# Moving the two transposes of 47 node sets of a graph network layer from TensorE to a DRAM round trip and VectorE block turns

## The chip, the cores and the metric

The kernel runs on one core of a Trainium2 chip. The metric is the time on the device of one execution, in microseconds (us). The engines of the core are TensorE (PE in the profile, with its weight loads as PEld), VectorE (DVE), ScalarE (ACT), GpSimd (POOL) and SyncE (SP, which here only issues DMA transfers and reads numbers into its registers). Each engine works through its own list of instructions in order and waits on semaphores.

## The reference

The reference is one layer of a graph network with 6250 nodes of 256 features and 206250 edges, sorted by target node.

```python
h = jnp.maximum(_layernorm(x, axis=-1), 0.0)
polarity = jnp.clip(edge_attr[:, 0:1], 0.0, 1.0)
raw = edge_attr[:, 1:]
e = jax.nn.relu(raw @ W_e1.T + b_e1) @ W_e2.T + b_e2
edge_emb = (e * (polarity + 0.01)) @ W_le.T + b_le
msg = jax.nn.relu(h[src] + edge_emb)
aggr = jax.ops.segment_sum(msg, dst, num_segments=N)
g = (h + aggr) @ W_g1.T + b_g1
hn = (g - mean(g)) * rsqrt(var(g) + 1e-5) * ln_g + ln_b
out = x + relu(hn) @ W_g2.T + b_g2
```

All of it is in 32-bit floats. For each node the last three lines need the node's row turned twice: TensorE contracts over partitions, so `h + aggr` (nodes on partitions) must be turned to features on partitions ahead of the product with `W_g1`, and the normalised rows must be turned again ahead of the product with `W_g2`.

## The kernel before

Edges are worked on in tiles of 128. Two tiles make a unit; I call the work of one unit a **step**. Twelve steps make a group of 3072 edges, and there are 67 groups and a remainder. The order of all instructions is written out by a Python loop over the steps (`for u in range(LEAD, NU)`), which emits for each step, to all engines, what is due; each engine then runs its own list in that order.

In a step TensorE makes the second product of a unit (line 377, eight instructions, since a 32-bit product counts twice) into a bank of PSUM that ScalarE has filled with the offset (line 408). VectorE multiplies by the polarity and adds the gathered source rows (line 822, two instructions for a unit), and ScalarE takes the relu (line 833). GpSimd gathers the source rows by indirect DMA (line 740). In the last step of a group TensorE also makes the first layer of the edges of the next group (line 342; VectorE and ScalarE take it out of PSUM at lines 355 and 358) and the sums of the whole group by target node (line 873). ScalarE and VectorE put the sums together in `ms` (lines 893 and 894), and SyncE writes them to the DRAM tensor `sum_d` (`rows_out`, line 980, four copies, two of which are emitted one step after the group's end and two one step later).

A **node set** is 128 nodes. When the sums of all its groups are written, `far_work` does the rest for it, spread over the steps behind: load the node's rows and the sums (line 1013), add them (line 1016), and then six stages, put on a list by `at(now + ...)`: `turned` (two transposes on TensorE, line 177, copied from PSUM by ScalarE at line 181), `one` (product with `W_g1`, line 192, then VectorE's addition and statistics at lines 200 to 163), `rooted` (ScalarE, line 206), `normed` (VectorE, lines 211 and 212), `two` (two transposes on TensorE, line 218, and relu with `ln_g` and `ln_b` by ScalarE, line 222) and `three` (product with `W_g2`, line 231, addition at line 236, and the copy out at line 239). 47 node sets go this way: 42 with buffers of their own, five with buffers that were kept free (`msg` in the names); in the last three of these five, the fillers, `two` and `three` are left for the very end. The two last node sets go another way (`node_work`), with one turn on TensorE each.

What `soon(n, fn)` puts off runs at the end of exactly the step asked for, all of it; what `at(u, fn)` puts off runs one piece for a step, and not in the last or first step of a group.

The first 24 units are kept (`KEPT`) and finished later. Ten of them have their source rows from the start; of the others, `BY_ROW` units get their source rows row by row, through copies of 1 KB that SyncE issues after it has read the row numbers into registers (lines 777 and 782, four rows in every second step), and the rest by gathers of GpSimd that stand between the others.

Of the kernel before, what the change touches and what calls it, by code (L numbers as in the profile page):

```python
# [9 lines left out]
F32 = mybir.dt.float32  # L10
I32 = mybir.dt.int32
AF = mybir.ActivationFunctionType
# [5 lines left out]
P = 128  # L18
# [29 lines left out]
ROWS = 4  # L48
BY_ROW = 5
SEEDS = 3  # L50
# [54 lines left out]
def gnn_kernel(ctx: ExitStack, tc: tile.TileContext, x, src_c, src_r, dst_c, dst_r, pol_c, raw_t, w_e1t, w_e2,  # L105
# [64 lines left out]
    def finish_nodes(nd, ps, w, n):  # L170
# [44 lines left out]
        def second(hs):  # L215
# [9 lines left out]
            return nT, a  # L225

        def third(nT, xt):
            nT, a = nT
# [20 lines left out]

        return turn, first, root, scaled, second, third, load_x, offset  # L250

# [3 lines left out]
    with fast:  # L255
# [216 lines left out]
        w0 = early.enter_context(tc.tile_pool(name="w0", bufs=1))  # L472
        wle_s = w0.tile([P, 2, D], F32, name="wle_s")
        nc.sync.dma_start(out=wle_s, in_=vec(w_let))
        we2_s = w0.tile([P, 2, D], F32, name="we2_s")
        nc.scalar.dma_start(out=we2_s, in_=vec(w_e2))
# [20 lines left out]
        dst_f = w0.tile([P, NT], F32, name="dst_f")  # L497
        be2_b = w0.tile([P, 2, P], F32, name="be2_b")

# [114 lines left out]


        wg1_s = const.tile([P, 2, D], F32, name="wg1_s")
        wg2_s = const.tile([P, 2, D], F32, name="wg2_s")
# [84 lines left out]
        with tc.tile_pool(name="hg", bufs=1) as hg_p, tc.tile_pool(name="ms", bufs=4) as ms_p, \  # L702
                tc.tile_pool(name="sel2", bufs=6) as sel2_p, tc.tile_pool(name="ab", bufs=2) as ab_p, \
                tc.tile_pool(name="nh", bufs=2) as nh, tc.tile_pool(name="nd", bufs=3) as nd, \
                tc.tile_pool(name="nk", bufs=1) as nk:
            base_i = nk.tile([1, NG * S], I32, name="base_i")
# [246 lines left out]
            whole_units = {}  # L953
            ready, fillers = [], []
            left = {w: set(groups_of(w)) for w in range(NW) if groups_of(w)[-1] < FAR}
# [45 lines left out]
            def far_work(w, nd=nd, nh=nh, ab_p=ab_p, filling=False):  # L1001

                box = {}
                turn, first, root, scaled, second, third, load_x, offset = finish_nodes(nd, ps, w, P)

# [9 lines left out]
                def add(i):  # L1015
                    nc.vector.tensor_add(box["h"], box["h"], box["ab"][:, i, :])
# [44 lines left out]
            def node_work(w, spread_now=False):  # L1061
# [4 lines left out]
                far_apart = (3, 5, 4) if gs[-1] < NG - 3 else (2, 3, 2)  # L1066
                turn, first, root, scaled, second, third, load_x, offset = finish_nodes(nd, ps, w, n)

# [205 lines left out]
def any_order(tc, dram, v):  # L1274
# [7 lines left out]
    with tc.tile_pool(name="sc", bufs=1) as sc, tc.tile_pool(name="sk", bufs=2) as sk, \  # L1282
# [93 lines left out]
        def nodes(w, n):  # L1376
            ac = sk.tile([P, D], F32, name="ac_a")
            nc.sync.dma_start(out=ac[:n], in_=acc_d[bass.ds(w * P, n), :])
            turn, one, root, scaled, two, three, load_x, offset = v["finish_nodes"](sk, Fresh(), w, n)
            xt = load_x()  # L1380
            offset(xt)
            three(two(scaled(root(one(turn(ac))))), xt)
# [68 lines left out]
```

## Time and profile before

| | |
|---|---|
| median of three runs | 2704.74 us (2699.62 to 2708.85) |
| the profiled execution | 2698.25 us, of which 2696.1 us from its first to its last instruction |
| mean granted clock of TensorE | 0.973 |
| busy, of the span | TensorE 94%, weight loads 62%, GpSimd 58%, VectorE 48%, ScalarE 48% |
| moved by DMA | 331.78 MB, 123 GB/s in the mean |

A row of the timeline gives the start, the length, the engine, the line, the operation with what it writes and reads, and how many instructions were merged; in brackets stands how long the engine had been idle ahead of it, and what ended that. A row of the groups gives the count, the busy time (overlaps counted once), the mean length of one in ns, and the idle time ahead of them with what ended most of it. SPq is SyncE's list of DMA issues; its time is the time of issuing, not of the transfer.

### The profile page before, as it was taken

The page shows a single profiled execution, that of the slowest core. Times are in us where ns is not written, and L with a number is a line of the kernel's source. Part 1 is how long each engine was busy: PE and PEld are TensorE (multiplying, and loading weights), DVE is VectorE, ACT ScalarE, POOL GpSimd, SP SyncE. Part 2 cuts the span into 40 slices and gives each one's busy share as a digit, 9 for nine tenths or more (in the row PEclk, how much of TensorE's full clock was granted, in tenths as well). Part 3 has the DMA queues.
Part 4 walks back from the last instruction along what each step waited for, and adds up shares of the span by engine and source line. Part 5 has one row for each costly group of instructions (what it writes and reads, how often), then busy time and mean ns, then how long its engine had stood idle before and what let it go on. Part 6 is the DMA issues. An engine that isn't in the chain of part 4 may idle for free.

```text
span 2696.1 us, 55548 instructions
## 1 busy us (share of the span) xinstructions
PE 2538.4 (94%) x19998; PEld 1664.0 (62%) x19998; DVE 1304.9 (48%) x2984; ACT 1290.8 (48%) x2414; POOL 1557.0 (58%) x1664
## 2 busy tenths in 40 slices
PE   9889999999999999999999999999999999999998
PEld 6455655665665666565666666566656665666665
DVE  6446545444444444444444444444444444545454
ACT  6345544444444444444444445444445444545544
POOL 7655555555555555555565555555555555555652
PEclk9889999999999989999999999999999999999999
DMA  9433434343444434434434444443444444434442
GB/s 296 152 93 115 121 116 128 116 123 114 119 121 123 125 105 125 120 115 119 130 109 123 124 118 121 124 117 117 124 121 120 125 121 122 119 115 128 122 120 58
DMA packets 145846, 331.78 MB, mean 123 GB/s; under 512 B 37129, under 2 KB 73836, under 8 KB 144812
## 3 DMA queue, kind: packets, MB, share of 16 engines
q0 software_dynamic: 76896, 210.08, 27.3%
q1 hardware_dynamic: 67368, 114.79, 13.5%
q10 hardware_dynamic: 1300, 3.29, 0.4%
q8 instruction: 160, 2.62, 0.4%
q14 instruction: 122, 1.00, 0.1%
HBM read 306.25 MB, written 34.08 MB: 126 GB/s over the span
## 4 chain that ended last, share of the span: by engine, by line
PE 78%; issue 10%; DVE 5%; ACT 4%; DMA 1%; POOL 1%; another core or an unknown queue 0%; DVEq 0%; SPq 0%; POOLq 0%; ACTq 0%
PE pz L377 40%; PE pz L342 20%; PE pz L873 14%; DVE hg L822 2%; PE pz L192 1%; ACT hg L833 1%; PE pz L231 1%; DVE hx L822 1%; ACT pz L408 1%; ACT hx L833 1%; POOL hg L740 1%; PE pz L218 1%; DVE hs L212 1%; DMA hx<-hb_d,src_s 0%; PE pz L177 0%
## 5 line engine op out<-in xcount | busy, mean ns | idle before, releaser
L377 PE MATMUL pz<-wc_s,e 128*128 128x256 f32 x6448 | 1450.7, 382 | 4.9 <-ACT pz L408 1.8
L377 PEld LDWEIGHTS pz<-wc_s,e 128*128 128x128 f32 x6448 | 1215.0, 191 | 203.5 <-issue 36.0
L740 POOL DMA_INDIRECT hg<-hb_d,src_s x976 | 927.1, 950 | 683.6 <-issue 210.6
L740 POOL DMA_INDIRECT hx<-hb_d,src_s x606 | 573.8, 947 | 400.5 <-issue 134.9
L342 PE MATMUL pz<-raw,we_s 64*32 64x512 f32 x6448 | 627.9, 642 | 82.2 <-issue 48.7
L822 DVE SCALAR_TENSOR_TENSOR hg<-pz,pol_s,hg 128x256 f32<-128x256 f32 x962 | 413.9, 477 | 414.8 <-issue 225.8
L833 ACT ACTIVATE hg<-hg 128x512 f32<-128x512 f32 x481 | 300.9, 626 | 445.4 <-DVE hg L822 365.9
L342 PEld LDWEIGHTS pz<-raw,we_s 64*32 64x32 f32 x6448 | 155.3, 111 | 510.8 <-issue 350.0
L355 DVE TENSOR_SCALAR e<-pz,vecs 128x512 f32<-128x512 f32 x395 | 284.4, 748 | 356.0 <-remote 184.6
L408 ACT ACTIVATE pz<-bc_s 128x512 f32<-128x512 f32 x782 | 452.7, 585 | 0.0
L358 ACT ACTIVATE e<-pz,vecs 128x512 f32<-128x512 f32 x411 | 266.0, 684 | 331.9 <-remote 161.5
L822 DVE SCALAR_TENSOR_TENSOR hx<-pz,pol_s,hx 128x256 f32<-128x256 f32 x602 | 260.9, 478 | 280.0 <-issue 129.5
L833 ACT ACTIVATE hx<-hx 128x512 f32<-128x512 f32 x300 | 188.0, 627 | 314.1 <-DVE hx L822 266.7
L873 PE MATMUL pz<-hg,sel 64*32 64x256 f32 x3848 | 306.2, 393 | 30.5 <-issue 12.7
L873 PEld LDWEIGHTS pz<-hg,sel 64*32 64x32 f32 x3848 | 133.6, 108 | 161.4 <-issue 141.6
L873 PE MATMUL pz<-hx,sel 64*32 64x256 f32 x2408 | 208.4, 387 | 18.6 <-issue 8.5
L894 DVE TENSOR_TENSOR ms<-ms,pz 128x256 f32<-128x256 f32 x68 | 28.6, 421 | 297.1 <-ACT ms L893 297.1
L893 ACT ACTIVATE ms<-pz 128x256 f32<-128x256 f32 x68 | 26.0, 383 | 274.5 <-PE pz L873 273.6
L873 PEld LDWEIGHTS pz<-hx,sel 64*32 64x32 f32 x2408 | 90.0, 107 | 90.8 <-issue 77.1
L803 DVE SCALAR_TENSOR_TENSOR sel<-iota_w,zero_c,rel 128x256 f32<-128x256 f32 x202 | 92.2, 476 | 0.0
L231 PE MATMUL pz<-wg_s,nT 128*128 128x256 f32 (+1 forms) x176 | 45.3, 380 | 0.0
L192 PE MATMUL pz<-wg_s,hT 128*128 128x256 f32 (+1 forms) x176 | 45.3, 380 | 0.0
(136 smaller groups left out, 698.2 us busy)
## 6 DMA issues: line engine op xcount, KB each, us to landing
raw<-in_raw_t_dram SPq DMA_DIRECT2D x99, 512.0 KB
hg<-hb_d,src_s POOLq DMA_INDIRECT x976
hg<-hb_d SPq DMA_DIRECT2D x768, 1.0 KB
sum_d<-zero_d SPq DMA_DIRECT2D x47, 256.0 KB
ab<-sum_d SPq DMA_DIRECT2D x42, 256.0 KB
hx<-hb_d,src_s POOLq DMA_INDIRECT x606
sum_d<-ms SPq DMA_DIRECT2D x264, 32.0 KB
hx<-hb_d SPq DMA_DIRECT2D x512, 1.0 KB
```

Of the source, the lines that this page charges most:

```text
L192: z = nc.tensor.matmul(ph[:n, 0, :], aT[:, c, :n], wg1_s[:, c, :], start=c == 0 and not bias_by_pe, stop=c == 1)
L231: z = nc.tensor.matmul(po[:n, 0, :], nT[:, c, :n], wg2_s[:, c, :], start=c == 0, stop=c == 1)
L342: z[c] = nc.tensor.matmul(bank[s, c].tile[j * W:(j + 1) * W].rearrange("p a b -> p (a b)"), we1_s[s * F:(s + 1) * F, c * P + j * W:c * P + ...
L355: a = nc.vector.tensor_scalar(e1[b][:, c, :], pe, be1_s[:, c:c + 1], 0.0, op0=ALU.add, op1=ALU.max)
L358: a = nc.scalar.activation(e1[b][:, c, :], pe, AF.Relu, bias=be1_s[:, c:c + 1])
L377: z = nc.tensor.matmul(bank.tile[:, i, :], e1[b][:, c, k:k + P], wc_s[:, c, :], start=not seeded and i == c == 0, stop=c == 1, skip_group_ ...
L408: a = nc.scalar.activation(bank.tile, bc_s, AF.Copy)
L740: g = nc.gpsimd.indirect_dma_start(out=hg[u][:, i, :], out_offset=None, in_=hb_d, in_offset=bass.IndirectOffsetOnAxis(ap=src_s[:, 2 * u + ...
L803: nc.vector.scalar_tensor_tensor(sel[g][:, k * S:k * S + n, :], iota_w.rearrange("p (o w) -> p o w", o=1).to_broadcast([P, n, W]), zero_c, ...
L822: product = nc.vector.scalar_tensor_tensor(hg[u][:, i, :], bank.tile[:, i, :], pol_s[:, 2 * u + i:2 * u + i + 1], hg[u][:, i, :], op0=ALU. ...
L833: done[u] = product, nc.scalar.activation(hg[u], hg[u], AF.Relu)
L873: z = nc.tensor.matmul(acc[g][h][j * W:(j + 1) * W, :], sel[g][h * F:(h + 1) * F, k * S + j, :], m[h * F:(h + 1) * F, j % 2, :], start=k = ...
```

## The change

`far_work` no longer turns on TensorE. `first_out` writes the 128 x 256 rows to one of eight DRAM buffers (`turn_d`); `in_blocks` reads them back by four DMA issues, one for each quarter of the partitions, in pieces of 32 floats (128 bytes), so that in the tile `pm` each 32 x 32 block stands where its turned block belongs; `turned` is one VectorE instruction that turns all 32 x 32 blocks. The same round trip (`second_out`, `in_blocks`, `second_turned`) replaces `two`, and the relu with `ln_g` and `ln_b` then goes from SBUF to SBUF (`relu_of`). The first turn changes for all 47 node sets; the second for 44, since the three fillers keep `two` on TensorE. The two stages that issue DMA are put off by `soon`, the others by `at`. `BY_ROW` is four instead of five, so 1024 rows are copied singly instead of 1280, and one more kept unit is gathered by GpSimd (two indirect DMAs). Two weights and a bias that only the start needs are in a pool that is closed early, which makes room for `pm`.

```diff
-BY_ROW = 5
+BY_ROW = 4
...
+    turn_d = [dram.tile([P, D], F32, name=f"turn_d{i}") for i in range(8)]
...
+        def relu_of(nT):
+            for c in range(2):
+                a = nc.scalar.activation(nT[:, c, :], nT[:, c, :], AF.Relu, bias=lnb_s[:, c:c + 1],
+                                         scale=lng_s[:, c:c + 1])
+            return nT, a
...
+                def out_rows(a):
+                    box["d"] = turn_d[len(turned_rows) % len(turn_d)]
+                    turned_rows.append(w)
+                    nc.sync.dma_start(out=box["d"], in_=a)
+
+                def in_blocks():
+                    box["pm"] = pm.tile([P, 2 * S, W], F32, name="pm")
+                    rows = box["d"].rearrange("(b i) (c a j) -> a i c b j", i=W, a=S, j=W)
+                    for q in range(S):
+                        nc.sync.dma_start(out=box["pm"][q * W:(q + 1) * W].rearrange("i (c b) j -> i c b j", c=2),
+                                          in_=rows[q])
+
+                def blocks_turned(name, pool):
+                    t = pool.tile([P, 2, P], F32, name=name)
+                    nc.vector.transpose(t.rearrange("p c n -> p (c n)"), box["pm"].rearrange("p q j -> p (q j)"))
+                    return t
+
+                def first_out():
+                    at_last(box)
+                    out_rows(box["h"])
+
                 def turned():
-                    at_last(box)
-                    box["hT"] = turn(box["h"], nh, "hT")
+                    box["hT"] = blocks_turned("hT", nh)
...
+                def second_out():
+                    out_rows(box["hs"])
+
+                def second_turned():
+                    box["nT"] = relu_of(blocks_turned("nT", nd))
+
                 def two():
                     box["nT"] = second(box["hs"])
...
-                stages = [turned, one, rooted, normed, two, three]
+                line = [(first_out, 2, True), (in_blocks, 3, True), (turned, 1, False), (one, 1, False),
+                        (rooted, 1, False), (normed, 1, False), (second_out, 2, True), (in_blocks, 3, True),
+                        (second_turned, 2, False), (three, 0, False)]
+                if filling:
+                    line = line[:6]

                 def run(i):
-                    stages[i]()
-                    if i < len(stages) - (3 if filling else 1):
-                        at(now + (2, 1, 1, 2, 3)[i], lambda: run(i + 1))
+                    line[i][0]()
+                    if i < len(line) - 1:
+                        if line[i + 1][2]:
+                            soon(line[i][1], lambda: run(i + 1))
+                        else:
+                            at(now + line[i][1], lambda: run(i + 1))
...
-                    fillers.append(stages[-2:])
-                at(now + 12, lambda: run(0))
+                    fillers.append((two, three))
+                soon(12, lambda: run(0))
```

How the order moves is seen best in one group. Its steps are counted from 0 to 11. On TensorE, before, from the end of a group's sums to the second transposes, behind step 7 of the next group (`pz` with its number is a PSUM bank; the two rows that read one `e_10x` are two steps):

```order
L873 MATMUL pz_151<-hg_874,sel_142 32x256
L377 MATMUL pz_146<-wc_s,e_102 128x256 x4
L377 MATMUL pz_148<-wc_s,e_102 128x256 x4
L177 MATMUL pz_147<-ident,stb 128x128 x2
L377 MATMUL pz_150<-wc_s,e_103 128x256 x4
L377 MATMUL pz_144<-wc_s,e_103 128x256 x4
L192 MATMUL pz_151<-wg_s,hT 128x256 x2
L377 MATMUL pz_149<-wc_s,e_104 128x256 x4
L377 MATMUL pz_145<-wc_s,e_104 128x256 x4
L377 MATMUL pz_146<-wc_s,e_105 128x256 x4
L377 MATMUL pz_148<-wc_s,e_105 128x256 x4
L218 MATMUL pz_147<-ident,hs 128x128 x2
```

And now (lines have moved by 5 to 10: 883 is 873, 384 is 377, 238 is 231, 193 is 192):

```order
L883 MATMUL pz_159<-hg_889,sel_150 32x256
L384 MATMUL pz_154<-wc_s,e_110 128x256 x4
L384 MATMUL pz_156<-wc_s,e_110 128x256 x4
L384 MATMUL pz_155<-wc_s,e_111 128x256 x4
L384 MATMUL pz_158<-wc_s,e_111 128x256 x4
L238 MATMUL pz_157<-wg_s,nT 128x256 x2
L384 MATMUL pz_152<-wc_s,e_112 128x256 x4
L384 MATMUL pz_153<-wc_s,e_112 128x256 x4
L193 MATMUL pz_159<-wg_s,hT 128x256 x2
```

The transposes are gone; the product with `W_g1` has moved from behind step 3 to behind step 5, and behind step 3 now stands the product with `W_g2` of the node set before.

On VectorE, now, from step 1 to the statistics (832 is 822, 813 is 803, 243 is 236, 201 is 200):

```order
L832 SCALAR_TENSOR_TENSOR hx_120<-pz_156,pol_s,hx_120 128x256 x2
L1042 STREAM_TRANSPOSE nT<-pm 128x256
L832 SCALAR_TENSOR_TENSOR hx_119<-pz_155,pol_s,hx_119 128x256 x2
L832 SCALAR_TENSOR_TENSOR hg_891<-pz_158,pol_s,hg_891 128x256 x2
L243 TENSOR_TENSOR ot<-pz_157,xt_8469 128x256
L832 SCALAR_TENSOR_TENSOR hg_892<-pz_152,pol_s,hg_892 128x256 x2
L1042 STREAM_TRANSPOSE hT<-pm 128x256
L832 SCALAR_TENSOR_TENSOR hx_124<-pz_153,pol_s,hx_124 128x256 x2
L201 TENSOR_TENSOR hs<-pz_159,rows_b 128x256
```

The second turn of a set stands behind step 1, the first turn of the next set behind step 4, one step ahead of TensorE's use of `hT`.

On SyncE, now, behind the group's end (990 is 980, 251 is 244, 787 and 792 are 777 and 782):

```order
L251 DMA xt_9185<-in_x_dram 128x256
L990 ISA
L990 DMA sum_d<-ms 32x256
L990 ISA
L990 DMA sum_d<-ms 32x256
L1037 DMA pm<-turn_d_68 32x8x32 x4
L787 TENSOR_LOAD list_5910
L792 ISA
L792 DMA hx_122<-hb_d 1x256
```

The four reads in blocks stand behind the last two of the four copies of the group's sums and ahead of the next four single rows, all on the one list of SyncE; the write to `turn_d_68` was issued at the end of the group before.

More of the change, by code (lines that the diff above doesn't have):

```diff
@@ L248, in offset @@
             nc.vector.scalar_tensor_tensor(xt[:n], xt[:n], zero_c[:n], bg2_b[:n], op0=ALU.add, op1=ALU.add)
-        return turn, first, root, scaled, second, third, load_x, offset
+        return turn, first, root, scaled, second, relu_of, third, load_x, offset
     NU = 2 * NB
@@ L1003, in far_work @@
                 box = {}
-                turn, first, root, scaled, second, third, load_x, offset = finish_nodes(nd, ps, w, P)
+                turn, first, root, scaled, second, relu_of, third, load_x, offset = finish_nodes(nd, ps, w, P)
                 def h_of_x():
@@ L1378, in nodes @@
             nc.sync.dma_start(out=ac[:n], in_=acc_d[bass.ds(w * P, n), :])
[L1379 removed]
+            turn, one, root, scaled, two, _, three, load_x, offset = v["finish_nodes"](sk, Fresh(), w, n)
             xt = load_x()
```

15 lines of the change are left out of this document (9 added, 6 removed).

## The prediction

> I expect the changed kernel to be **slower, about 2770 us**: it takes some 38 us of work off TensorE, and makes TensorE wait, 47 times, for a turn that VectorE reaches too late.
>
> **What bounds the kernel now.** I read the page first: the busy shares and the chain that ended last.
>
> ```profile
> PE 2538.4 (94%) x19998; PEld 1664.0 (62%) x19998; DVE 1304.9 (48%) x2984; ACT 1290.8 (48%) x2414; POOL 1557.0 (58%) x1664
> PE 78%; issue 10%; DVE 5%; ACT 4%; DMA 1%; POOL 1%; another core or an unknown queue 0%; DVEq 0%; SPq 0%; POOLq 0%; ACTq 0%
> ```
>
> TensorE is busy 94% of the span and makes up 78% of the chain. Whatever it need not do is a gain, and whatever it must wait for is a loss, as long as nothing else ends later. So I read one group on its timeline.
>
> ```profile
> 1032.53 0.38 PE L177 MATMUL pz<-ident,stb 128*128 128x128 f32 x2
> 1032.75 3.62 PE L377 MATMUL pz<-wc_s,e 128*128 128x256 f32 x16
> 1036.21 1.03 PE L192 MATMUL pz<-wg_s,hT 128*128 128x256 f32 x4
> 1037.07 7.07 PE L377 MATMUL pz<-wc_s,e 128*128 128x256 f32 x32
> 1044.34 0.44 PE L218 MATMUL pz<-ident,hs 128*128 128x128 f32 x2 [0.20 <-DVE hs L212]
> 1044.62 5.34 PE L377 MATMUL pz<-wc_s,e 128*128 128x256 f32 x24
> ...
> 1071.21 0.38 PE L177 MATMUL pz<-ident,stb 128*128 128x128 f32 x2
> ```
>
> The group takes 1071.21 - 1032.53 = 38.7 us. The last of 16 products starts 3.62 - 0.38 = 3.24 us behind the first, so products start every 0.216 us, and a step of eight takes 1.73 us. There is no gap between rows but the 0.20 us at line 218.
>
> **What the change takes away.** The first transposes start at 1032.53 and the next product at 1032.75: the pair costs 0.22 us. Of the 32 products from 1037.07, the last starts at 1037.07 + 7.07 - 0.38 = 1043.76; the next product starts at 1044.62, where 0.22 would do: the second pair, with its wait for VectorE, costs 0.64 us.
>
> ```profile
> L177 PE MATMUL pz<-ident,stb 128*128 128x128 f32 x84 | 16.0, 273 | 0.0
> L218 PE MATMUL pz<-ident,hs 128*128 128x128 f32 (+1 forms) x88 | 18.9, 297 | 8.2 <-DVE hs L212 3.0 <-issue 1.6 <-DVE rs L211 1.5
> L177 PE MATMUL pz<-ident,msg 128*128 128x128 f32 x10 | 1.9, 272 | 0.0
> L218 PE MATMUL pz<-ident,msg 128*128 128x128 f32 x10 | 2.0, 284 | 0.7 <-ACT ms L893 0.7
> L181 ACT ACTIVATE hT<-pz 128x256 f32<-128x256 f32 x42 | 15.3, 365 | 0.0
> ```
>
> 84 + 10 first transposes are 47 pairs, all removed: 47 x 0.22 = 10.3 us. Of the second, 88 + 10 less four of the last two sets and six of the fillers, 44 pairs go: 44 x 0.64 = 28.2 us. Together **38.5 us**, if TensorE stays the bound. ScalarE's copy at line 181 goes too (15.3 us, off the path); its relu stays, now from SBUF.
>
> **What it adds beside other work.** VectorE gets 91 turns of 128 x 256. No turn is in this trace; the nearest rows are an addition of that size and one of twice the size.
>
> ```profile
> L1016 DVE TENSOR_TENSOR stb<-stb,ab 128x256 f32<-128x256 f32 x84 | 35.0, 416 | 1.3 <-DMA ab<-sum_d 1.1
> L843 DVE TENSOR_TENSOR msg<-msg,bc_s 128x512 f32<-128x512 f32 x7 | 4.8, 682 | 0.0
> ```
>
> I take 0.45 us, between bounds of 0.42 and 0.68: 41 us on an engine that is busy 48%. The turn's own length is paid only where TensorE waits for it, below. [...]
>
> The one more kept unit costs GpSimd two gathers:
>
> ```profile
> L740 POOL DMA_INDIRECT hx<-hb_d,src_s x606 | 573.8, 947 | 400.5 <-issue 134.9
> ```
>
> At 947 ns each they are 1.9 us; GpSimd is idle 42% of the span, and its gathers run ahead of their use. If that cover were gone, these would be the cost. SyncE loses 256 single rows and gets 47 + 44 = 91 writes and 364 block reads.
>
> ```profile
> 1025.48 1.62 SPq L782 DMA_DIRECT2D hx<-hb_d  x4
> 1029.91 1.83 SPq L980 DMA_DIRECT2D sum_d<-ms  x2
> 1031.79 0.42 SPq L244 DMA_DIRECT2D xt<-in_x_dram  x1
> 1033.59 1.79 SPq L980 DMA_DIRECT2D sum_d<-ms  x2
> 1035.95 4.90 SPq L782 DMA_DIRECT2D hx<-hb_d  x4
> SPq L324 <- PE pz L342: 329.2, 63, 26.0
> SPq L980 <- DVE ms L894: 265.3, 62, 26.9
> SPq L980 <- DMA sum_d<-ms: 134.6, 111, 3.0
> ```
>
> An issue takes 1.62 / 4 = 0.4 us when SyncE is quick and 4.90 / 4 = 1.2 us when it is slow (this slow stretch comes behind the sums in this group). Ten issues for a node set are 4 to 12 us. SyncE's slack is its waits for TensorE and VectorE, 329.2 + 265.3 = 594.5 us, or 8.9 us for each of 67 groups. So on the mean it keeps up, narrowly while rows are copied singly. The second turn has much time: it is written behind step 7, read behind step 10, and wanted behind step 1 of the next group, with the long last step between. I cost it at nothing; were SyncE late there by more than that step, TensorE would wait at `three` instead.
>
> **The wait it adds.** The first turn has no such room. `in_blocks` is issued behind the last two copies of `sum_d`, which end at 1033.59 + 1.79 = 1035.4. Four issues end 1.6 to 4.9 us later, at 1037.0 to 1040.3. For the landing, the bounds are these: the copy of 1033.59 waits for that of 1029.91, so a landing takes at most 3.7 us there, and 134.6 / 111 = 1.2 us of waiting on the mean. For the pieces of 128 bytes:
>
> ```profile
> q1 hardware_dynamic: 67368, 114.79, 13.5%
> ```
>
> Its columns are packets, MB and share: 13.5% of 2696.1 us is 364 us of all 16 engines. By bytes 0.131 MB take 0.4 us; if each of 1024 pieces cost as much as a mean packet here, 5.5 us. So `pm` is there between 1038.6 and 1049.5. I take about 1041.5, nearer the lower end, because the pieces are far smaller than the mean packet (1.7 KB). [...] No row here shows pieces of 128 bytes.
>
> VectorE must also get there. `hT` is turned behind step 4 on its list, and step 4 comes late:
>
> ```profile
> 1036.46 0.88 DVE L822 SCALAR_TENSOR_TENSOR hg<-pz,pol_s,hg 128x256 f32<-128x256 f32 x2 [0.85 <-issue]
> 1038.19 0.18 DVE L163 BATCH_NORM_AGGREGATE mv<-st 128x2 f32<-128x6 f32 x1
> 1041.70 0.88 DVE L822 SCALAR_TENSOR_TENSOR hg<-pz,pol_s,hg 128x256 f32<-128x256 f32 x2 [3.33 <-PE pz L377]
> 1042.50 0.87 DVE L822 SCALAR_TENSOR_TENSOR hx<-pz,pol_s,hx 128x256 f32<-128x256 f32 x2
> 1043.66 0.63 DVE L212 TENSOR_SCALAR hs<-hs,mv,rs 128x256 f32<-128x256 f32 x1
> 721.48 1.66 DVE L822 SCALAR_TENSOR_TENSOR hg<-pz,pol_s,hg 128x256 f32<-128x256 f32 x4 [3.32 <-PE pz L377]
> ```
>
> TensorE's products of step 4 end at about 1037.07 + 1.73 + 0.17 = 1039.0, yet VectorE starts on them at 1041.70, after 3.33 us of idling; in the group of 721.48 it idles 3.32 us at the same place. Why the news is late the profile doesn't show; that it is late is borne out by line 212, whose end at 1044.29 is what TensorE waits 0.20 us for at line 218. Today only line 218 hangs on it, and loses those 0.20 us. After the change `hT` does. The turn can start at 1042.5, and `hT` is ready at about 1042.95.
>
> TensorE wants it behind step 5. The products of step 5 end their starts at 1037.07 + 16 x 0.216 = 1040.53; the pair of first transposes is gone (0.22 earlier), and the four products of line 231 now stand where the four of line 192 stood: about 1040.3. The wait is 1042.95 - 1040.3 = **2.6 us**, and every later step stands behind it.
>
> Its bounds: nothing, if VectorE reaches step 4 in time and `pm` lands by 1039.8; and 1049.5 + 0.45 - 1040.3 = 9.7 us, if every landing took the longest. Sets near the start and the end, and groups where the news comes sooner, wait less; I take **2.2 us** for the mean of 47 sets, 103 us.
>
> **The sum.** 2698.25 - 38.5 + 103 = 2763 us for the profiled execution. It lay 6.5 us under the median of the runs (2704.74), so I write **2770 us**.
>
> **Rivals.** *The turn comes in time.* If VectorE's idling at step 4 goes with the new order, step 4 ends at 1039.0 + 0.8 and the turn at 1040.3, just when TensorE wants it. Then the 38.5 us are won: 2704.74 - 38.5 = 2666 us. For it: the idling is not explained, and the work before it changes. Against it: it stands in both groups shown, to 0.01 us.
>
> *The wait eats the gain.* At 38.5 / 47 = 0.8 us a set the two cancel, 2705 us; it takes a `pm` by 1040.6 and a prompt step 4.
>
> *The stops slow the clock.* Where TensorE stopped twice for short, its clock was halved behind it:
>
> ```profile
> 971.85 1.06 PE L342 MATMUL pz<-raw,we_s 64*32 64x512 f32 x9 [0.87 <-DVE hx L822]
> 973.43 12.10 PE L342 MATMUL pz<-raw,we_s 64*32 64x512 f32 x54 [0.52 <-issue]
> 975.00:985.00 10.00, 10.00 (x57) 2.48 (x63) 3.61 (x5) 3.33 (x5) 4.79 (x6) 0.50 0.31 91
> 1056.62 4.56 PE L342 MATMUL pz<-raw,we_s 64*32 64x512 f32 x63 [0.80 <-issue]
> ```
>
> The window's granted clock is 0.50, and 54 products took 12.10 us where 63 elsewhere took 4.56: 12.10 - 54 x 4.56 / 63 = 8.2 us lost. If a third of the 47 stops did half of that, 16 x 4 = 64 us more: 2834 us. [...]
>
> **Chances.** My forecast, 2735 to 2805 us, 0.38; the slowed clock or landings near their upper bound 0.14; the cancelling 0.15; the turn in time 0.33. A measurement of this kernel can't tell less than 0.3% (8 us) from no change: faster 0.33, same 0.15, slower 0.52. The range must hold the faster case, so it goes from 2662 to 2835 us; the forecast's own is 2735 to 2805.
>
> **What would show it.** Line 193 on TensorE with 2 to 3 us of idling ahead of it, ended by VectorE's line 1042, in most of 47 places; VectorE's line 832 of step 4 still with over 3 us ahead of it, or line 1042 itself waiting for the DMA of `pm`, which tells whether VectorE or the transfer is late; line 177 gone and line 219 left with 10 instructions; line 1042 with 91 instructions of 0.42 to 0.68 us; no idling at line 238. The prediction is wrong if line 193 idles less than 0.8 us, or if TensorE's pauses move to line 349 (342) because SyncE brings `raw` late.

## The result, and the profile after

The changed kernel takes 2776.56 us (median, 2766.15 to 2781.46) against 2705.93 us for the kernel before: a ratio of 1.0268, 95% interval 1.0244 to 1.0291. It is slower by 71 us, near the 2770 us that were forecast. The profiled execution lasts 2781.46 us, with a span of 2779.7 us and a mean granted clock of 0.960 (0.973 before). The two profiled executions lie 83.2 us apart, more than the medians, since the one before was the fastest of its kernel's and this one the slowest; what follows accounts for these 83 us.

Line numbers of the changed kernel are 5 to 10 higher: 384 is 377, 349 is 342, 883 is 873, 832 is 822, 193 is 192, 238 is 231; 1042 is the new turn. The page after, busy shares and chain:

```profile
PE 2538.2 (91%) x19816; PEld 1680.8 (60%) x19816; DVE 1341.6 (48%) x3075; ACT 1287.2 (46%) x2367; POOL 1561.3 (56%) x1666
PE 79%; issue 11%; DVE 4%; ACT 2%; DMA 2%; POOL 1%; SPq 1%; DVEq 0%; another core or an unknown queue 0%; POOLq 0%
q1 hardware_dynamic: 178964, 138.41, 17.2%
```

TensorE has 182 instructions fewer and is busy as long as before (2538.2 us for 2538.4), because other instructions take longer; the 83.6 us of the longer span are idle time. The groups of lines say where it idles, and that the second products (377, now 384) and the product with `W_g1` (192, now 193) have become longer, though their work is unchanged (before, then after):

```profile
L377 PE MATMUL pz<-wc_s,e 128*128 128x256 f32 x6448 | 1450.7, 382 | 4.9 <-ACT pz L408 1.8 <-issue 1.6 <-ACT rs L1179 1.2
L342 PE MATMUL pz<-raw,we_s 64*32 64x512 f32 x6448 | 627.9, 642 | 82.2 <-issue 48.7 <-DVE hg L822 15.3 <-DVE hx L822 5.2
L192 PE MATMUL pz<-wg_s,hT 128*128 128x256 f32 (+1 forms) x176 | 45.3, 380 | 0.0
```

```profile
L384 PE MATMUL pz<-wc_s,e 128*128 128x256 f32 x6448 | 1461.9, 386 | 9.0 <-issue 5.9 <-ACT rs L1222 2.4 <-ACT pz L415 0.6
L349 PE MATMUL pz<-raw,we_s 64*32 64x512 f32 x6448 | 613.3, 641 | 69.7 <-issue 45.0 <-DVE hg L832 12.4 <-DVE hx L832 3.0
L193 PE MATMUL pz<-wg_s,hT 128*128 128x256 f32 (+1 forms) x176 | 59.8, 470 | 78.2 <-DVE hT L1042 73.4
L193 PE MATMUL pz<-wg_s,msg 128*128 128x256 f32 x20 | 5.4, 395 | 4.2 <-DVE msg L1042 2.1 <-issue 2.1
L219 PE MATMUL pz<-ident,msg 128*128 128x128 f32 x6 | 1.3, 292 | 0.7 <-ACT ms L903 0.7
L238 PE MATMUL pz<-wg_s,nT 128*128 128x256 f32 (+1 forms) x176 | 45.4, 380 | 0.8 <-issue 0.7
```

Line 193 idles 78.2 + 4.2 = 82.4 us; nothing idled there before. Busy times of groups overlap, so I also followed TensorE's work in order and gave each instruction only the time by which it moved the end of the work (own time), and the idle time ahead of it:

| work | before, own + idle, us | after, own + idle, us | difference, us |
|---|---|---|---|
| transposes | 30.0 + 8.9 | 1.9 + 0.9 | -36.1 |
| product with `W_g1`, `hT` | 38.2 + 0.0 | 59.1 + 78.2 | +99.1 |
| second products (377, 384) | 1415.6 + 4.9 | 1441.3 + 9.0 | +29.8 |
| first layer (342, 349) | 622.8 + 82.2 | 608.3 + 69.7 | -27.0 |
| sums (873, 883) | 369.8 + 50.0 | 365.0 + 68.2 | +13.4 |
| product with `W_g2`, `nT` | 38.3 + 0.0 | 38.5 + 0.8 | +1.0 |
| both products of the five `msg` sets | 8.7 + 0.0 | 9.4 + 4.2 | +4.9 |
| rest | 20.8 | 18.8 | -2.0 |
| sum | 2690.2 | 2773.3 | +83.1 |

One set, TensorE and VectorE on the timeline:

```profile
1096.84 3.62 PE L384 MATMUL pz<-wc_s,e 128*128 128x256 f32 x16
1103.15 1.13 PE L193 MATMUL pz<-wg_s,hT 128*128 128x256 f32 x4 [2.69 <-DVE hT L1042]
1101.87 0.87 DVE L832 SCALAR_TENSOR_TENSOR hx<-pz,pol_s,hx 128x256 f32<-128x256 f32 x2 [4.40 <-PE pz L384]
1102.66 0.43 DVE L1042 STREAM_TRANSPOSE hT<-pm 128x256 f32<-128x256 f32 x1
```

Of the 16 products from 1096.84 the first eight are step 4; they end at about 1098.7. VectorE starts on them at 1101.87, and the turn of 0.43 us stands right behind. TensorE, done with step 5 at 1100.46, waits 2.69 us. This lateness of what VectorE is told by TensorE's semaphore I call **late news**. In another set step 4 comes sooner, and the blocks are late in its place:

```profile
1185.76 0.88 DVE L832 SCALAR_TENSOR_TENSOR hx<-pz,pol_s,hx 128x256 f32<-128x256 f32 x2 [2.43 <-ACT pz L415]
1187.45 0.45 DVE L1042 STREAM_TRANSPOSE hT<-pm 128x256 f32<-128x256 f32 x1 [0.81 <-DMA pm<-turn_d]
1182.58 2.57 SPq L1037 DMA_DIRECT2D pm<-turn_d  x4
1187.95 1.13 PE L193 MATMUL pz<-wg_s,hT 128*128 128x256 f32 x4 [2.13 <-DVE hT L1042]
  DMA pm<-turn_d: 29.5, 17
```

SyncE's four issues end at 1185.15, the blocks have landed at 1187.45: 2.3 us behind the last issue. By the last row, from the view of line 1042 alone, its turns waited for blocks in 17 places, 29.5 us in all. Followed set by set, 49.3 of the 82.4 us of stops stand in sets whose turn starts right behind step 4, and the other 33.1 us in sets where VectorE idles between step 4 and the turn.

The second products grew because the clock was halved behind some of the stops. Here are two stops of the same length, in stretches of 3.41 us (columns: length, then busy time and count of TensorE, weight loads, VectorE, ScalarE, GpSimd, then the granted clock, the DMA share and GB/s):

```profile
1098.83:1102.24 3.41, 1.63 (x8) 1.09 (x6) 0.37 (x1) 0.00 (x0) 1.10 (x3) 1.00 0.36 93
1102.24:1105.66 3.42, 2.51 (x12) 2.23 (x13) 2.65 (x8) 2.23 (x4) 1.81 (x2) 1.00 0.39 117
1228.54:1231.95 3.41, 0.74 (x4) 0.34 (x3) 1.49 (x4) 0.58 (x2) 1.18 (x2) 1.00 0.28 91
1231.95:1235.36 3.41, 3.41 (x9) 2.69 (x9) 1.53 (x5) 1.65 (x4) 0.95 (x1) 0.50 0.55 163
1231.74 1.91 PE L193 MATMUL pz<-wg_s,hT 128*128 128x256 f32 x4 [2.67 <-DVE hT L1042]
```

The stop of 2.69 us ahead of 1103.15 is spread over two of these stretches, and the clock stays at 1.00. The stop of 2.67 us ahead of 1231.74 lies in one, and in the next the clock is 0.50: the four products take 1.91 us instead of 1.13. In the clock records of the trace all 49 halved stretches start on one grid of 3.41 us, and all but one last one, two or four of its steps. 18 of the sets have one within 7 us behind line 193, all of them after stops of 2.07 us or more; in the kernel before none had one.

### The profile page after: what moved, and what is told of

The parts are those of the page before. It is cut to its first block, busy times and chain, and to the rows that moved or that the text cites. A ratio compares the mean times of both kernels' runs of the same rounds, so it can differ in the third digit from the quotient of the medians.

```text
span 2779.7 us, 55073 instructions
## 1 busy us (share of the span) xinstructions
PE 2538.2 (91%) x19816; PEld 1680.8 (60%) x19816; DVE 1341.6 (48%) x3075; ACT 1287.2 (46%) x2367; POOL 1561.3 (56%) x1666
## 3 DMA queue, kind: packets, MB, share of 16 engines
q1 hardware_dynamic: 178964, 138.41, 17.2%
## 4 chain that ended last, share of the span: by engine, by line
PE 79%; issue 11%; DVE 4%; ACT 2%; DMA 2%; POOL 1%; SPq 1%; DVEq 0%; another core or an unknown queue 0%; POOLq 0%
PE pz L384 43%; PE pz L349 20%; PE pz L883 12%; PE pz L193 2%; DVE hg L832 1%; PE pz L238 1%; POOL hg L750 1%; DVE hx L832 1%; ACT pz L415 1%; ACT hg L843 1%; DVE hT L1042 1%; DMA sum_d<-ms 0%; DMA pm<-turn_d 0%; ACT hx L843 0%; POOL hx L750 0%
## 5 line engine op out<-in xcount | busy, mean ns | idle before, releaser
L384 PEld LDWEIGHTS pz<-wc_s,e 128*128 128x128 f32 x6448 | 1242.7, 194 | 222.7 <-issue 41.3
L750 POOL DMA_INDIRECT hx<-hb_d,src_s x616 | 583.9, 948 | 439.6 <-issue 136.1
L349 PE MATMUL pz<-raw,we_s 64*32 64x512 f32 x6448 | 613.3, 641 | 69.7 <-issue 45.0
L883 PE MATMUL pz<-hg,sel 64*32 64x256 f32 x3808 | 297.4, 398 | 39.5 <-issue 26.6
L883 PE MATMUL pz<-hx,sel 64*32 64x256 f32 x2448 | 227.2, 389 | 27.5 <-issue 18.7
L883 PEld LDWEIGHTS pz<-hg,sel 64*32 64x32 f32 x3808 | 139.7, 110 | 154.2 <-issue 135.9
L193 PE MATMUL pz<-wg_s,hT 128*128 128x256 f32 (+1 forms) x176 | 59.8, 470 | 78.2 <-DVE hT L1042 73.4
L193 PEld LDWEIGHTS pz<-wg_s,hT 128*128 128x128 f32 (+1 forms) x176 | 34.7, 217 | 97.9 <-DVE hT L1042 87.4
```

Source lines behind the costliest of these rows:

```text
L193: z = nc.tensor.matmul(ph[:n, 0, :], aT[:, c, :n], wg1_s[:, c, :], start=c == 0 and not bias_by_pe, stop=c == 1)
L349: z[c] = nc.tensor.matmul(bank[s, c].tile[j * W:(j + 1) * W].rearrange("p a b -> p (a b)"), we1_s[s * F:(s + 1) * F, c * P + j * W:c * P + ...
L384: z = nc.tensor.matmul(bank.tile[:, i, :], e1[b][:, c, k:k + P], wc_s[:, c, :], start=not seeded and i == c == 0, stop=c == 1, skip_group_ ...
L750: g = nc.gpsimd.indirect_dma_start(out=hg[u][:, i, :], out_offset=None, in_=hb_d, in_offset=bass.IndirectOffsetOnAxis(ap=src_s[:, 2 * u + ...
L883: z = nc.tensor.matmul(acc[g][h][j * W:(j + 1) * W, :], sel[g][h * F:(h + 1) * F, k * S + j, :], m[h * F:(h + 1) * F, j % 2, :], start=k = ...
```

## The experiments

Chips differ, and so each kernel is compared only with the kernel before on its own chip: 2707.56 us for the first four kernels below, 2103.51 us for the next four, 2672.94 us (the chip of the first four, at another time) for the two after them, 2700.56 us for the last two.

**One turn alone.** In the list of stages, first with the first turn only, then with the second only; there `turned_by_pe` turns on TensorE as before, the fillers end at `line[:4]`, and the first stage is put off by `at` again (these edits are left out):

```diff
-                        (rooted, 1, False), (normed, 1, False), (second_out, 2, True), (in_blocks, 3, True),
-                        (second_turned, 2, False), (three, 0, False)]
+                        (rooted, 1, False), (normed, 2, False), (two, 3, False), (three, 0, False)]
...
-                line = [(first_out, 2, True), (in_blocks, 3, True), (turned, 1, False), (one, 1, False),
+                line = [(turned_by_pe, 2, False), (one, 1, False),
```

> Only the first turn goes by DRAM and VectorE; the second is made by TensorE as before. Theory A (TensorE stands at line 193 because hT is late, and its clock drops behind some of the stops): the stops stay, 41 of them of about 2 us, and the 28.2 us of the second transposes come back, so 2777 + 28 = about 2805 us. Rival B (the loss is spread: 455 more DMA issues and 1024 small pieces for each turn slow SyncE and the transfers for all): half of the traffic is gone, so about half of the loss, 2706 + 35 - 10 = about 2730 us.

Measured: 2772.06 us, ratio 1.0224 (1.0191 to 1.0256).

> Only the second turn goes by DRAM and VectorE; the first is made by TensorE as before. Theory A: no stop at line 193, only the gain of the second transposes is left, 2706 - 28 = about 2678 us, and the granted clock is back at 0.973. Rival B: half of the traffic costs half of the loss, about 2730 us.

Measured: 2718.22 us, ratio 1.0033 (1.0016 to 1.0051). Line 193 with the first turn only, then lines 193 and 349 with the second only:

```profile
L193 PE MATMUL pz<-wg_s,hT 128*128 128x256 f32 (+1 forms) x176 | 60.4, 474 | 88.1 <-DVE hT L1042 62.4 <-issue 25.7
```

```profile
L193 PE MATMUL pz<-wg_s,hT 128*128 128x256 f32 (+1 forms) x176 | 45.3, 380 | 0.0
L349 PE MATMUL pz<-raw,we_s 64*32 64x512 f32 x6448 | 679.6, 683 | 101.3 <-issue 61.7 <-DVE hg L832 19.8 <-DVE hx L832 5.7
```

The first turn alone brings the whole loss, with 88.1 us of stops; the second brings none of them. That speaks for theory A against B. But both numbers of theory A are off, the first by 33 us to the good, the second by 40 us to the bad. The second turn alone should have won 28 us and lost 11: TensorE idles 19.1 us more at line 349 than before (101.3 against 82.2), and the first layer is busy 51.7 us longer (679.6 against 627.9): 172.5 us of it lie in halved stretches, 97.3 us before. The clock of that profiled run, the slowest of its eight, is 0.959. Followed in order as above, its transposes and their waits cost 25.8 us less, its last steps with first layer and sums 47.5 us more. The gain is real up to the last step of the group, and is paid back in it; why the last step pauses more is not shown.

What holds `hT` back differs between the two kernels. In the changed kernel VectorE starts on step 4 over 1 us late in 23 of 41 sets; with the first turn only it does so in 3, and the blocks come last. The idle time ahead of line 1042, and one set:

```profile
  DMA pm<-turn_d: 82.6, 36
1100.83 2.57 SPq L1037 DMA_DIRECT2D pm<-turn_d  x4
1102.17 0.88 DVE L832 SCALAR_TENSOR_TENSOR hx<-pz,pol_s,hx 128x256 f32<-128x256 f32 x2 [0.85 <-issue]
1105.14 0.45 DVE L1042 STREAM_TRANSPOSE hT<-pm 128x256 f32<-128x256 f32 x1 [2.09 <-DMA pm<-turn_d]
```

So late blocks alone are enough for stops of this size, on the chip of the kernel before. Their lateness depends on SyncE's list: the last of the four issues ends 0.6 us before TensorE is done with step 5 here, and 1.5 us before that in the changed kernel (medians). With a landing about 2.1 us behind the issue and the turn of 0.45 us, the blocks alone would stop TensorE for about 1 us a set in the changed kernel, some 50 us in all; this is an estimate.

**The first turn two steps later.**

```diff
-line = [(first_out, 2, True), (in_blocks, 3, True), (turned, 1, False), (one, 1, False),
+line = [(first_out, 2, True), (in_blocks, 5, True), (turned, 1, False), (one, 1, False),
```

> All of the change, but the first turn and all that follows it come two steps later, so TensorE wants hT 3.5 us later than in the changed kernel. Theory A: the stops at line 193 were 2.1 us, at most 3.4, so they are gone, and the whole gain comes out: 2706 - 38 = about 2668 us, with line 193 idle for less than 5 us. Rival B: the traffic is the same, so about 2770 us.

Measured: 2722.82 us, ratio 1.0064 (1.0045 to 1.0084).

```profile
L193 PE MATMUL pz<-wg_s,hT 128*128 128x256 f32 (+1 forms) x176 | 49.5, 404 | 25.4 <-DVE hT L1042 23.3 <-issue 1.2 <-DVE hx L832 0.6
L349 PE MATMUL pz<-raw,we_s 64*32 64x512 f32 x6448 | 628.6, 640 | 85.3 <-issue 54.3 <-DVE hg L832 13.4 <-DVE hx L832 2.7
```

The stops fall from 78.2 us (61.1 us in a later run of the changed kernel, below) to 25.4 us, most of the loss goes, and so timing is its cause and not the traffic, which is the same (B falls). They don't end: most sets still stop for 0.2 to 1.0 us, and in all of them the turn starts right behind VectorE's other work. So 3.5 us of room were not enough, and theory A as I had put it was short.

**Four units row by row, and nothing else.**

```diff
-BY_ROW = 5
+BY_ROW = 4
```

> The kernel before with four units row by row instead of five and nothing else. Theory A: within 3 us of before, 2703 to 2709 us, since SyncE and GpSimd have room for either. Rival C (the single rows matter, to SyncE or to the gathers of GpSimd): off by more than 8 us to one side.

Measured: 2704.14 us, ratio 0.9991 (0.9977 to 1.0005). This part of the change does nothing that can be measured.

**The blocks read one step earlier.** This kernel and the next three ran on the chip where the kernel before takes 2103.51 us.

```diff
-line = [(first_out, 2, True), (in_blocks, 3, True), (turned, 1, False), (one, 1, False),
+line = [(first_out, 1, True), (in_blocks, 4, True), (turned, 1, False), (one, 1, False),
```

> All of the change, but the four reads in blocks of the first turn are issued one step earlier, ahead of the last two copies of the sums. Theory A1 (the blocks are late as well as the news): VectorE stood 29.5 us for pm in 17 places; with pm 1.7 us earlier these waits go, and some 25 to 30 us of TensorE's stops with them, 2745 to 2755 us, while the sets held by the late step 4 keep their stops of 2.5 us. Theory A2 (only the late news of step 4 counts): 2770 to 2780 us.

Measured: 2116.84 us, ratio 1.0055 (1.0038 to 1.0071).

**Other gates for the gathers.** The table lets the gathers of a unit go once TensorE has done a certain step; seven of its twelve entries become one to three steps later.

```diff
-GATES = {0: (-1, 3), 2: (-1, 5), 4: (-1, 6), 6: (-1, 8), 8: (-1, 9), 10: (-1, 10), 12: (-1, 12), 14: (-1, 15), 16: (-1, 17), 18: (-1, 18), 20: (0, 1), 22: (0, 2)}
+GATES = {0: (-1, 6), 2: (-1, 7), 4: (-1, 8), 6: (-1, 9), 8: (-1, 10), 10: (-1, 10), 12: (-1, 12), 14: (-1, 15), 16: (-1, 17), 18: (-1, 18), 20: (0, 4), 22: (0, 5)}
```

> All of the change, and the table that lets GpSimd's gathers go behind certain steps is changed, so that the gathers of three units that began behind step 1 of a group begin behind step 4. Theory G (TensorE's news to VectorE is held back while GpSimd issues a run of gathers, until about 1.5 us behind the last of them): step 4 on VectorE is then in time, step 7 or so is late in its place; the stops at line 193 shrink to what the blocks cost, about 1 us, and the time falls by 40 us or more, to 2740 us or less. Rival S (SyncE's traffic behind the sums holds the news back, or it is the group's phase): VectorE's idling ahead of step 4 stays over 2.5 us and the time at 2770 to 2780 us.

Measured: 2242.61 us, ratio 1.0668 (1.0641 to 1.0694). Lines 349 and 193, and what VectorE's line 1042 idled for, first with the early read, then with the other gates (reads where the change has them):

```profile
L349 PE MATMUL pz<-raw,we_s 64*32 64x512 f32 x6448 | 374.8, 600 | 20.5 <-DVE hg L832 10.4 <-ACT e L365 4.8 <-DMA raw<-in_raw_t_dram 2.9
L193 PE MATMUL pz<-wg_s,hT 128*128 128x256 f32 (+1 forms) x176 | 47.6, 394 | 9.6 <-DVE hT L1042 9.5
  DMA pm<-turn_d: 23.8, 16
```

```profile
L193 PE MATMUL pz<-wg_s,hT 128*128 128x256 f32 (+1 forms) x176 | 59.9, 471 | 94.7 <-DVE hT L1042 94.5
  DMA pm<-turn_d: 130.0, 47
```

On this chip the first layer is busy 375 us instead of 601 to 628, and VectorE's step 4 is in time in nearly every group (it starts 0.09 us behind the end of step 4, in the median), with either gates. So the gates told nothing there, as theory G has no late news to move. But the chip shows the other half of the wait by itself: with the news in time, the blocks alone stop TensorE for 94.7 us; read one step earlier, for 9.6 us (these two kernels differ in the gates too).

**TensorE kept at work in the wait.**

```diff
+            if n == P and not bias_by_pe:
+                for c in range(4):
+                    nc.tensor.matmul(ph[:n, 0, :], ident, wg1_s[:, 0, :], start=True, stop=True)
```

> All of the change, and TensorE makes eight more instructions (four products of the identity with a weight, 1.73 us, into the bank that line 193 then writes anew) ahead of line 193, so that it isn't idle for most of its wait. Its output is the same. Theory K (the clock is halved because TensorE stood): the waits add up to max(1.73, stop) for each set, 19 us more than the stops alone, but no product behind them is slow, which is worth about 40 us (25.7 at line 384 and 21 at line 193 less its own start-up): about 2755 us, and no halved clock within 7 us behind line 193. Rival (the clock is halved for another reason, the transfers or the turn on VectorE): about 2795 us, with as many slow stretches behind line 193 as before.

Measured: 2228.65 us, ratio 1.0593 (1.0573 to 1.0614). The expected times were for the slower chips; what can be compared is the kernel with the other gates on this chip, whose stops were of the same kind. Lines move by 3 (387 is 384, 196 is 193), and 194 is the added work:

```profile
L387 PE MATMUL pz<-wc_s,e 128*128 128x256 f32 x6448 | 1434.7, 382 | 5.1 <-ACT pz L418 5.0
L194 PE MATMUL pz<-wg_s,ident 128*128 128x256 f32 x384 | 91.4, 381 | 3.0 <-DVE hx L835 3.0
L196 PE MATMUL pz<-wg_s,hT 128*128 128x256 f32 (+1 forms) x176 | 51.6, 418 | 37.5 <-DVE hT L1045 37.3
```

With 384 more instructions TensorE is done 14 us sooner than with the other gates. The granted clock is 0.992 against 0.978, line 196 takes 418 ns against 471, and 6 sets have a halved stretch within 7 us behind them against 21. That speaks for theory K: it is the standing still that halves the clock. It was compared with a kernel that differs in its gates too, so the size is not settled.

**The first turn three steps later.** The same edit with 6 for 5.

> All of the change, the first turn and all behind it three steps later. With two steps later the idle time at line 193 was still 25 us, 0.55 us in most sets. Theory A: one step more ends it (under 5 us idle), and with the slow products behind it some 30 us are won: about 2690 us. What then is left of the distance to 2668 us is in the last step of the groups (line 349), which costs more or less according to where its short pauses fall. Rival: the wait moves on to line 238 or to the second turn's blocks, about 2720 us.

Measured: 2316.59 us, ratio 1.1007 (1.098 to 1.1034).

```profile
L238 PE MATMUL pz<-wg_s,nT 128*128 128x256 f32 (+1 forms) x176 | 73.2, 557 | 147.5 <-ACT nT L230 147.5
L193 PE MATMUL pz<-wg_s,hT 128*128 128x256 f32 (+1 forms) x176 | 45.9, 383 | 4.1 <-DVE hT L1042 4.1
  DMA pm<-turn_d: 197.1, 43
```

Line 193 is down to 4.1 us, and the rival came true: the second turn's blocks are now read behind those of the first, all eight issues in one step, and line 238 waits 147.5 us for them. This order was not tried on a slower chip.

**The change and the kernel before once more.**

> The changed kernel once more, beside the kernel before, since the last four kernels ran on a chip where the kernel before takes 2103.5 us. On such a chip, theory T (TensorE's news comes in time there, and only the blocks are late): line 193 idles about 95 us, as in the run with other gates, and the time is 2215 to 2245 us against 2103 us; the four reads in blocks land after TensorE wants hT in most sets. Rival: without late news the change is no slower there, 2080 to 2110 us. On a chip where the kernel before takes 2705 us: 2765 to 2785 us again.

Measured: 2723.68 us against 2672.94 us, ratio 1.018 (1.0144 to 1.0216).

> The kernel before, for its profile on this chip. Where it takes 2103 us: VectorE's step 4 is in time (its idling of 3.3 us ahead of it is gone), the halved clock is rare (a granted clock of 0.99), and the first layer and the sums take about 390 and 183 us as in the other kernels of that chip. Where it takes 2705 us: as in the profile shown.

Measured: 2669.28 us, one run. The chip was that of the first four kernels, where the kernel before now took 1.3% less.

```profile
L193 PE MATMUL pz<-wg_s,hT 128*128 128x256 f32 (+1 forms) x176 | 54.3, 435 | 61.1 <-DVE hT L1042 39.6 <-issue 14.9 <-DVE hx L832 6.5
```

The change is slower again, by less: 61.1 us of stops for 78.2, and 11 sets with a halved stretch behind them for 18. VectorE's step 4 is over 1 us late in 16 of 41 sets, for 23. On the chip of 2103 us neither kernel has a profile, so what the change itself does there was not measured.

**The gates once more, on a chip of 2700 us.**

> The kernel with the gathers of three units begun behind step 4 instead of step 1, once more, for a chip where the kernel before takes about 2700 us. Theory G (a run of gathers holds TensorE's news back): VectorE's step 4 is in time and step 7 or 8 late in its place; the stops at line 193 that waited for step 4 go, those that waited for the blocks stay. Rival S: step 4 is late as before, and the time is that of the changed kernel, 1.8 to 2.7% over the kernel before. Where the kernel before takes 2103 us, nothing is told by it: 2240 us as before.

Measured: 3067.15 us, ratio 1.1362 (1.1334 to 1.1389). Lines 193 and 349, and the last step of a group with GpSimd's gathers in it:

```profile
L193 PE MATMUL pz<-wg_s,hT 128*128 128x256 f32 (+1 forms) x176 | 48.4, 397 | 14.2 <-DVE hT L1042 7.6 <-issue 5.4 <-DVE msg L855 1.2
L349 PE MATMUL pz<-raw,we_s 64*32 64x512 f32 x6448 | 928.7, 750 | 187.8 <-issue 140.5 <-DVE hg L832 23.1 <-DVE hx L832 5.2
1158.60 0.88 DVE L832 SCALAR_TENSOR_TENSOR hg<-pz,pol_s,hg 128x256 f32<-128x256 f32 x2 [1.36 <-ACT pz L415]
1167.69 0.88 DVE L832 SCALAR_TENSOR_TENSOR hg<-pz,pol_s,hg 128x256 f32<-128x256 f32 x2 [3.35 <-issue]
1165.04 0.95 POOL L750 DMA_INDIRECT hg<-hb_d,src_s  x1 [0.30 <-issue]
1175.17 2.04 PE L349 MATMUL pz<-raw,we_s 64*32 64x512 f32 x3 [0.41 <-issue]
1178.02 0.90 PE L349 MATMUL pz<-raw,we_s 64*32 64x512 f32 x1 [0.80 <-issue]
1179.31 0.95 POOL L750 DMA_INDIRECT hx<-hb_d,src_s  x1 [0.30 <-issue]
```

Theory G holds: with the run of gathers moved, VectorE's step 4 is in time (1158.60; over 1 us late in none of 41 sets, for 23 in the changed kernel), and a later step is late in its place (1167.69, after 3.35 us of idling, behind a run of six gathers whose last began at 1165.04). The stops at line 193 fall from 78.2 to 14.2 us. Not all of that is the news: the blocks are issued sooner too, 2.0 us before TensorE is done with step 5 for 1.5 (medians). The price was not foreseen. The last step, from the first layer to the sums, lasts 23.2 us for 17.4, and in the rows shown TensorE makes one to three products at a time in it with pauses of 0.4 to 0.8 us between. Line 349 idles 187.8 us, and 426 us of its busy time lie in halved stretches; the clock is 0.914 in the mean of the run. More gathers begin in the last step (12.4 for 8.7 a group), but hardly more for each microsecond, so that they are the cause is not shown.

**The blocks one step earlier and the turn two steps later.** On the same chip:

```diff
-line = [(first_out, 2, True), (in_blocks, 3, True), (turned, 1, False), (one, 1, False),
+line = [(first_out, 1, True), (in_blocks, 6, True), (turned, 1, False), (one, 1, False),
```

> All of the change, with the reads in blocks of the first turn one step earlier and its turn on VectorE two steps later. Theory A: line 193 idles less than 5 us, and what the turn alone two steps later still lost there (25 us of idling and 10 us of slow products) is won: 0.6% over the kernel before becomes 0.5 to 1% under it, 2680 to 2693 us where the kernel before takes 2705 us. Where the kernel before takes 2103 us: 2065 to 2090 us, since with the early read alone line 193 idled 10 us. Rival: the reads ahead of the copies make the sums or the second turn late, and it is within 0.5% of the kernel before or above.

Measured: 2716.57 us, ratio 1.0067 (1.0043 to 1.0091).

```profile
L193 PE MATMUL pz<-wg_s,hT 128*128 128x256 f32 (+1 forms) x176 | 48.9, 400 | 30.6 <-DVE hT L1042 23.9 <-DVE hg L832 4.8 <-DVE hx L832 1.7
1042.49 0.88 DVE L832 SCALAR_TENSOR_TENSOR hx<-pz,pol_s,hx 128x256 f32<-128x256 f32 x2 [1.39 <-issue]
1043.61 0.87 DVE L832 SCALAR_TENSOR_TENSOR hx<-pz,pol_s,hx 128x256 f32<-128x256 f32 x2
1044.40 0.43 DVE L1042 STREAM_TRANSPOSE hT<-pm 128x256 f32<-128x256 f32 x1
```

A miss: line 193 keeps 30.6 us. The blocks are no longer the reason; nearly every turn of a set starts at once behind the step ahead of it (4 turns waited for blocks, 9.6 us in all). VectorE works through steps 5 and 6 late and back to back, and the turn is behind them. Moving the turn along VectorE's list doesn't help while the list itself runs late there. None of these kernels beats the kernel before.

## Why the prediction was right, point by point

**The total and its sign** came out as forecast, 2776.6 for 2770 us. The sum was nearer than its terms: it had 64.5 us for the profiled executions, where 83 were measured. The stops were put 20.6 us too long, the slowed clock (46.6 us) was not in it, the first layer took 27.0 us less and the sums 13.4 us more. That these nearly cancel is luck; that TensorE waits for `hT` at line 193, and that this costs more than the transposes did, was foreseen.

**What the change takes away**: 38.5 us were worked out, 36.1 us are gone from TensorE's own row. The step "if TensorE stays the bound" is the weak one. The kernel with the second turn only should have shown 28 us of gain and showed a loss of 11: what TensorE gains ahead of the last step it loses in that step, in pauses and in halved clock. The sum holds the idle time at line 342 to be fixed, and it is not.

**The turn on VectorE** is 0.43 to 0.45 us in all 91 places; 0.45 was taken.

**The four units row by row** cost nothing, as forecast: 0.9991.

**The second turn at nothing**: line 238 idles 0.8 us. Nor did `raw` come late: line 349 idles less than line 342 did. In the kernel with the first turn and all behind it three steps later it idles 147.5 us on the chip of 2103 us, where its blocks are read behind the long last step instead of ahead of it; that fits the cover that was named, but eight issues in one step were new there too.

**The wait it adds** was put at 2.6 us a set and 2.2 us on the mean, 103 us; measured are 82.4 us over 47 sets, 1.75 us each, 1.0 to 2.8 us in most. The mechanism was right for the larger part: line 832 of step 4 comes late, and `hT` right behind it. What I had not given enough weight is that the blocks are late too. For 17 of 91 turns `pm` came last, and with the news in time the blocks alone stopped TensorE for 88.1 us in the kernel with the first turn only. The prediction had them land at 1041.5, 1.2 us after TensorE wants `hT` and 1.0 us ahead of VectorE; in the set of 1187.95 they landed 1.6 us after, and behind VectorE. A prompt step 4 would have saved only part of the wait.

**The slowed clock** was left to a rival, 64 us by a third of the stops, and the sum had it at zero. It came: 18 of the sets have a halved stretch behind them, and the products at lines 193 and 384 cost 20.9 + 25.7 = 46.6 us more of their own time, the start behind each stop included (the four products at 1103.15 took 1.13 us at full clock, those at 1036.21 in the kernel before, with no stop ahead of them, 1.03 us). The row of two short stops that the prediction quoted was the right one to trust: here the clock was halved behind 18 stops of 2.07 to 3.38 us; a stop of 2.67 us in one stretch of the grid had it at 0.50 in the next, one of 2.69 us spread over two left it at 1.00. Shorter pauses went with a lower clock too: in the run with the other gates on a chip of 2700 us line 349 pauses 0.4 to 0.8 us at a time in the rows shown, 426 us of its busy time lie in halved stretches, and the mean clock is 0.914.

**The turn in time** (a third of the chances): in the changed kernel step 4's idling was not gone. It was gone on the chip of 2103 us and with the first turn only, and in both the blocks were late.

## What to carry to other kernels

Work that leaves the bounding engine is a gain only if what takes its place is ready when that engine wants it; read from the trace not when the new engine has room, but when it is told, and when its data has landed, and take the later of the two. Where the two lie close together, curing one leaves most of the wait: with the first turn only, step 4 was over 1 us late in 3 sets for 23, and 88.1 us of stops stood there even so. Short stops of TensorE cost more than their length in these runs: 82.4 us of them came with 46.6 us of longer products. Nor were pauses of under 1 us slack: behind two of 0.87 and 0.52 us the kernel before had a clock of 0.50. A moved step or gather that cures one wait can cost more in the next stage (with the other gates line 193 stops 14.2 us for 78.2, and line 349 idles 187.8 us for 69.7), so time the whole kernel and look at the stage behind the one that was cured.

## What the runs showed of the hardware

- **TensorE's news came late while GpSimd gathered.** In the kernel before, 311 of 1363 recorded updates of TensorE's semaphore came over 1 us behind the modelled end of the instruction that sends them; of VectorE's 1732 and ScalarE's 1369, two each. 234 of the 311 belong to the first layer, line 342. In the changed kernel a late update came 1.44 us, in the median, behind the end of the last gather of a run of six; with the run moved, step 4 was over 1 us late in none of 41 sets for 23, and in the set shown a later step started after 3.35 us of idling. On the chip of 2103 us it is absent (2 of 1476 in the kernel with the early read), and the first layer is shorter there; whether the late news is what makes it long elsewhere is not shown. Ends of matmuls are modelled in the trace, so whether TensorE's last writes or only its news were late is open, and so is why that chip is free of it.
- **The halved stretches lie on a grid of 3.41 us**, all 49 of the changed kernel's trace, which was divided along that grid, from 250 us on. Of the stretches at full speed with over 2.1 us of idle TensorE 17 of 18 were followed by a halved one, of those with 1.4 to 2.1 us 15 of 31, of those with under 0.5 us 1 of 485. The counts hang on where a product is taken to end: by the modelled ends, as in the windows above, they are 15 of 15, 14 of 25 and 1 of 544. In the kernel with the second turn only, where the pauses lie in the first layer, 15 of 16 stretches with over 1.4 us were, and 8 of 44 with 0.5 to 0.8 us.
- **The same kernel takes 2103 us on one chip and 2673 to 2708 us on others.** On the first, in the kernel with the early read, the first layer's busy time is 375 us, against 601 to 628 in the changed kernel and the kernel before on the others, and the sums take 305 us against 508 to 525; the second products have nearly the same pace (381 ns, and 382 in the kernel before). Neither of these two kernels has a profile on the first chip, and the early read none on another, so how much the chip changes the loss is open.
- **Pieces of 128 bytes**, 131 KB in 1024 pieces, land about 2.1 to 2.3 us behind the last of their four issues (medians of the turns that waited for them, changed kernel and first turn only); the prediction's upper bound was 5.5 us of transfer and 3.7 us of landing. Queue q1's share rose from 13.5 to 17.2% for a fifth more bytes and 2.7 times the packets.
